# Second layer of a two-layer network: where the softplus pieces, the direct products and TensorE's taps and sums stand among the steps

## The chip, the core and the metric

The kernel runs on one core of one Trainium2 chip. The time is that of one execution on the device, in microseconds (us); of several runs the median is taken. The engines are named as in the profile: PE is TensorE's matmul, PEld its weight load, DVE is VectorE, ACT is ScalarE, POOL is GpSimd, SP is SyncE, which issues the transfers here. Each engine works through its own instructions strictly in the order of the program; engines wait for each other by semaphores.

## What is computed

The input is 16 images of 128 channels with 56 x 56 pixels, all in 32-bit floats. The first layer is a block of window attention and an MLP; the change leaves it alone. The second layer, cut to what matters:

```python
y = conv3x3(x) + conv_b                       # 128 -> 128 channels
seq = y.reshape(B*H*W, 8, 16)                 # 8 tokens of 16 numbers
xi, z = split(seq @ in_proj.T)                # 32 and 32
xc = silu(causal_conv4(xi) + conv1d_b)
dt, Bm, Cm = split(xc @ x_proj.T)             # 1, 16, 16
dt = softplus(dt * dt_proj + dt_proj_b)       # 32
# over the 8 tokens, for 32 channels x 16 states:
h = exp(dt * A) * h + dt * Bm * xc
ys = sum over the states of h * Cm
ym = (ys + D * xc) * silu(z)
out = ym @ out_proj.T
return x + silu(group_norm(out))
```

## The kernel before

**Blocks.** `layer1` cuts each image into 7 blocks of 448 columns, 112 blocks in all, and works on them one after another. A block has 8 tokens and two halves `jp` of its channels, so token 1 to 7 times two halves gives 14 *steps*; the outer loop runs over blocks `i`, the inner over steps `k` from 0 to 13. No scheduler sets the order: the loop at the end of `layer1` issues the instructions, and `_chain` ties every instruction to the one before it on its engine. So the order of the source is the order on every engine.

**The recurrence in each step.** In this order of issue:
- `advance` (DVE): L946 multiplies the decay `a` by the state before, L947 adds the input. For the last token there is one instruction (L944) in place of the two.
- `inject` (DVE, L936): the input of a step 4 ahead, from `x` in PSUM and the gate `bb` in SBUF, into a tile `h`. `h` has four buffers, which are handed out in turn.
- `decay` (PE, L918): the exponent of a step 2 ahead, into one of two PSUM tiles `a`.
- `spread` (PE, L929): the input of a step 5 ahead, into the only PSUM tile `x`.
- `decay_exp` (ACT, L921): the exponential of `a` in place. `advance` two steps later reads it.
- `weigh` (POOL, L951), in odd steps: a token's `h` times the gate `cb`, into one of four tiles `cst`.

**The rest of the work** is dealt out by `work(i, k)`, which returns a list for PE (with the ACT instructions that belong to it), one for DVE and one for POOL; a step issues them after the recurrence, DVE's first, then PE's, then POOL's. `p` is the block at hand, `nxt` the next, `far` the one after that, `prev` the one before, `two` and `three` those two and three blocks back. Two PSUM banks, `pq[0]` and `pq[1]`, serve all of it:
- for `far`: `sequences` (L829, step 11) and `inner` for `xc` (L836, then a table load, two SiLU, and a load back to the table of Exp and Ln, step 12);
- for `nxt`: the rate's softplus in two halves. `rate` (PE L850, ACT L851 and L852), `rate_exp` (ACT L856, L857), `rate_log` (ACT L861, L862) and `rate_sum` (POOL L867 to L870, steps 6 and 8). Then `gate` (PE L876, ACT copies L880, two transfers to memory, step 3), `inner` for `zs` (step 4), `product` (POOL L896, step 10) and `direct` (PE L900), whose result `direct_mul` (DVE, two L905) uses for the first and last token;
- for `p`: `skip` (L966), which opens a sum in `pq[1]`, `gather` (L960, four matmuls for each token), which adds to it, `collect` (DVE L973), `gated` (POOL L976);
- for `prev`: the last gathers, `project_out` (PE L994, ACT copies L1002 and L1005, steps 5 and 6) and `statistics` (DVE L1021; a block with an odd number issues two, one in step 9 and one in step 10 of the block after it);
- for the next image: `convolve`, the 9 *taps* of the 3x3 convolution (L787, accumulated in `pq[0]`, steps 5 to 10), after the last one the copies L796 on ACT;
- once in each image: the group norm. Its variance (PE L1038, ACT L1039 and L1040) comes in step 5 of block 1 of the next image, `normalise` (a load, two long SiLU at L1061, a load) in step 12 of the same block, and the `store` steps on POOL (L1068) with the output transfers after it.

**Transfers.** SP issues them in the order of the program: `bring` reads the gates back, spread over the partitions, as `bb` and `cb`.

Before the change the list for a block reads, in step order: rates in 1 and 2, `rate_exp` in 2 and 3, `rate_log` in 3 and 4, taps 1, 1, 2, 2, 2, 1 in steps 5 to 10, gathers of tokens 1, 2, 3 in steps 8, 9, 10, and in step 13 `skip`, `gather` of token 4 and then `direct`, with `direct_mul` in step 1 of the block after it.

## Time and profile before

| what | value |
|---|---|
| median of 3 runs | 8841.8 us (8837.53 to 8855.01) |
| the profiled execution | 8843.74 us, its span 8841.9 us |
| granted clock of TensorE, mean | 0.966 |
| PE, PEld | 91%, 38% of the span |
| DVE, ACT, POOL | 88%, 63%, 80% of the span |
| second layer, first to last L944/L946 | 3250.8 to 8801.4 us |
| L946 waits for L921 (ACT), in the layer | 357.5 us, 232 times, longest 6.6 |
| L936 waits for L929 (PE) | 141.7 us, 234 times, longest 2.6 |
| L936 waits for the transfer of `bb` | 30.7 us, 12 times, longest 3.1 |

How to read the profile: the span runs from the program's first instruction to its last, on the engines' clocks. A line of a group has the source line, engine and operation, the tiles that it writes and reads, how often it ran, then its busy time and the mean duration of one, and last the idle time of the engine in front of it with what ended that. A line of a timeline has the start and the duration in us, then the same names; "x2" means that two neighbours were merged, and a wait stands in brackets at its end. Neighbours on one engine overlap by up to a tenth of a microsecond. A line of a table of windows has the stretch, its length, the busy time of each engine with its number of instructions, the granted clock, the busy share of the DMA engines and GB/s. A matmul in 32-bit floats shows as two instructions.

### The profile page before, as it was taken

The page shows a single profiled execution, that of the slowest core. Times are in us where ns is not written, and L with a number is a line of the kernel's source. Part 1 is how long each engine was busy: PE and PEld are TensorE (multiplying, and loading weights), DVE is VectorE, ACT ScalarE, POOL GpSimd, SP SyncE. Part 2 cuts the span into 40 slices and gives each one's busy share as a digit, 9 for nine tenths or more (in the row PEclk, how much of TensorE's full clock was granted, in tenths as well). Part 3 has the DMA queues.
Part 4 walks back from the last instruction along what each step waited for, and adds up shares of the span by engine and source line. Part 5 has one row for each costly group of instructions (what it writes and reads, how often), then busy time and mean ns, then how long its engine had stood idle before and what let it go on. Part 6 is the DMA issues. An engine that isn't in the chain of part 4 may idle for free.

```text
span 8841.9 us, 151450 instructions
## 1 busy us (share of the span) xinstructions
PE 8013.1 (91%) x52860; PEld 3322.9 (38%) x52860; DVE 7764.8 (88%) x10358; ACT 5603.8 (63%) x10516; POOL 7035.4 (80%) x5664
## 2 busy tenths in 40 slices
PE   6999999999999879999999999999999999999987
PEld 3444444444444433333333333333333333333332
DVE  7999999999999839898898988988988989889887
ACT  4776777777777636666655665665656665666654
POOL 5878888878888328888888888888888888888887
PEclk8999999999999989999999999999999999999997
DMA  2333333333333222333333333333333333333332
GB/s 62 85 85 89 87 87 87 86 87 89 87 86 88 76 61 80 93 90 83 90 90 83 91 83 99 84 88 93 87 85 86 88 92 91 82 98 85 87 89 69
DMA packets 764424, 757.86 MB, mean 86 GB/s; under 512 B 188688, under 2 KB 663952, under 8 KB 761616
## 3 DMA queue, kind: packets, MB, share of 16 engines
q1 hardware_dynamic: 763664, 748.18, 32.8%
q8 instruction: 422, 6.91, 0.3%
q14 instruction: 338, 2.77, 0.1%
HBM read 439.61 MB, written 102.76 MB: 61 GB/s over the span
## 4 chain that ended last, share of the span: by engine, by line
PE 31%; ACT 24%; DVE 21%; POOL 11%; issue 10%; DMA 1%; SPq 0%; ACTq 0%; POOLq 0%; DVEq 0%
PE pq L787 8%; PE a L918 8%; ACT a L921 5%; DVE a L946 5%; DVE lepe L460 4%; DVE h L947 4%; POOL xh L263 4%; PE pq L960 4%; POOL e L379 4%; PE x L929 3%; ACT L837 3%; DVE h L936 3%; POOL tap L261 2%; ACT L145 2%; DVE sst L363 2%
## 5 line engine op out<-in xcount | busy, mean ns | idle before, releaser
L951 POOL TENSOR_TENSOR cst<-h,cb 128x1792 f32<-128x1792 f32 x784 | 3129.4, 3996 | 855.1 <-DVE h L947 580.4
L921 ACT ACTIVATE a<-a 128x896 f32<-128x896 f32 x1568 | 1404.3, 900 | 1772.7 <-PE x L929 1174.8
L936 DVE TENSOR_TENSOR h<-x,bb 128x896 f32<-128x896 f32 x1568 | 1697.6, 1083 | 276.9 <-PE x L929 145.6
L918 PE MATMUL a<-dt,adec 32*128 32x448 f32 x6272 | 1659.7, 606 | 214.4 <-DVE h L947 213.5
L946 DVE TENSOR_TENSOR a<-a,h 128x896 f32<-128x896 f32 x1344 | 1466.3, 1091 | 358.1 <-ACT a L921 357.5
L460 DVE SCALAR_TENSOR_TENSOR lepe<-vpad,lep,lepe 128x448 f32<-128x448 f32 x2688 | 1718.4, 678 | 0.6
L929 PE MATMUL x<-dtx,amask 32*128 32x448 f32 x6272 | 1664.8, 608 | 25.5 <-DVE h L936 24.5
L947 DVE TENSOR_TENSOR h<-a,h 128x896 f32<-128x896 f32 x1344 | 1467.0, 1092 | 45.8
L379 POOL TENSOR_SCALAR e<-e,sst,zero 128x256 f32<-128x256 f32 x1568 | 861.6, 560 | 451.4 <-DVE sst L375 396.6
L369 ACT ACTIVATE e<-ps,sst 128x256 f32<-128x256 f32 x1568 | 728.8, 469 | 544.5 <-DVE sst L363 493.6
L787 PE MATMUL pq<-x1pad,conv 128*128 128x448 f32 x2016 | 942.8, 580 | 59.5 <-ACT gst L1039 32.5
L918 PEld LDWEIGHTS a<-dt,adec 32*128 32x128 f32 x6272 | 484.2, 188 | 1247.4 <-DVE h L947 578.4
L263 POOL TENSOR_TENSOR xh<-xh,tap 128x448 f32<-128x448 f32 x735 | 841.4, 1145 | 42.5
L960 PE MATMUL pq<-cst,sel 128*32 128x448 f32 x6272 | 750.9, 564 | 1.5 <-POOL cst L951 1.5
L401 PE MATMUL ptt<-ident,e 128*128 128x128 f32 x3136 | 546.4, 285 | 92.3 <-POOL e L379 75.2
L363 DVE TENSOR_REDUCE sst<-ps 128x2 f32<-128x512 f32 x784 | 540.4, 689 | 86.3 <-PE ps L357 63.8
L929 PEld LDWEIGHTS x<-dtx,amask 32*128 32x128 f32 x6272 | 485.0, 189 | 339.8 <-DVE h L936 333.7
L357 PE MATMUL ps<-sel,q 32*64 32x256 f32 x6272 | 540.8, 413 | 68.2 <-ACT e L369 61.7
L261 POOL TENSOR_SCALAR tap<-xpad,pos,zero 128x448 f32<-128x448 f32 x735 | 533.6, 726 | 34.4
L787 PEld LDWEIGHTS pq<-x1pad,conv 128*128 128x128 f32 x2016 | 349.2, 194 | 497.4 <-issue 441.9
L401 PEld LDWEIGHTS ptt<-ident,e 128*128 128x128 f32 x3136 | 367.9, 142 | 416.5 <-POOL e L379 238.0
L407 ACT COPY att<-ptt 128x512 f32<-128x512 f32 x784 | 458.6, 585 | 48.0 <-PE ptt L401 40.3
(164 smaller groups left out, 12292.7 us busy)
## 6 DMA issues: line engine op xcount, KB each, us to landing
sel<-kv SPq DMA_DIRECT2D x3136, 64.0 KB
bb<-db SPq DMA_DIRECT2D x336, 448.0 KB
cb<-dc SPq DMA_DIRECT2D x336, 448.0 KB
xpad<-x SPq DMA_DIRECT2D x32, 784.0 KB
x<-r SPq DMA_DIRECT2D x112, 224.0 KB
x1pad<-x SPq DMA_DIRECT2D x16, 1568.0 KB
db<-bs SPq DMA_DIRECT2D x112, 224.0 KB
dc<-cs SPq DMA_DIRECT2D x112, 224.0 KB
```

The lines of the kernel that those rows point to most:

```text
L263: nc.gpsimd.tensor_add(im["xh"][i], im["xh"][i], held["tap"])
L379: nc.gpsimd.tensor_scalar(e, e, im["st", w][:, 2, p : p + 1], zero, ALU.mult, ALU.add)
L460: nc.vector.scalar_tensor_tensor(out, src, lep[:, k : k + 1], acc, ALU.mult, ALU.add)
L787: nc.tensor.matmul(pc, lhsT=conv[:, k, :], rhs=pad[:, 8 * i + dy : 8 * i + dy + 8, dx : dx + W], start=(k == 0), stop=(k == 8),)
L918: nc.tensor.matmul(a[:, k, :], lhsT=adec[rows, l4, :], rhs=p["dt"][rows, h, :], start=True, stop=True)
L921: nc.scalar.activation(p["a", l, jp], p["a", l, jp], AF.Exp)
L929: nc.tensor.matmul(x[:, k, :], lhsT=mask[rows, l4, :], rhs=p["dtx"][rows, h, :], start=True, stop=True)
L936: nc.vector.tensor_mul(p["h", l][:, own(jp), :], px["x"], weight)
L946: nc.vector.tensor_mul(a, a, before)
L947: nc.vector.tensor_add(p["h", l][:, own(jp), :], a, p["h", l][:, own(jp), :])
L951: nc.gpsimd.tensor_mul(c, p["h", l], p["gate", 1, l].unsqueeze(1).to_broadcast([P, 4, BLK]))
L960: nc.tensor.matmul(py[32 * j : 32 * j + 32], lhsT=sel[:, l4, :], rhs=p["c", l][:, j, :], start=False, stop=(l % 4 == 3), skip_group_check= ...
```

## The change

All of it is in `work`; no instruction is added, removed or resized.

```diff
         if p:
-            if k == 1:
+            if k == 0:
                 dve.append(partial(direct_mul, p))
             if k == 7:
                 pe.append(partial(skip, p, 0))
-            if k in (8, 9, 10):
-                pe.append(partial(gather, p, k - 7))
+            if k in (8, 9, 11):
+                pe.append(partial(gather, p, min(k - 7, 3)))
             if k == 12:
                 dve.append(partial(collect, p, 0))
             if k == 13:
+                if nxt:
+                    pe.append(partial(direct, nxt))
                 pe += [partial(skip, p, 1), partial(gather, p, 4)]
                 pool.append(partial(gated, p, 0))
...
             if k in (1, 2):
                 pe.append(partial(rate, nxt, k - 1))
-            if k in (2, 3):
-                pe.append(partial(rate_exp, nxt, k - 2))
-            if k in (3, 4):
-                pe.append(partial(rate_log, nxt, k - 3))
+            if k in (2, 6):
+                pe.append(partial(rate_exp, nxt, k // 4))
+            if k in (5, 7):
+                pe.append(partial(rate_log, nxt, k // 2 - 2))
...
             if k == 10:
                 pool.append(partial(product, nxt))
-            if k == 13:
+            if k == 13 and not p:
                 pe.append(partial(direct, nxt))
 
         if p and k in (5, 6, 7, 8, 9, 10) and p["b"] + 1 < NB:
-            taps = {5: (0,), 6: (1,), 7: (2, 3), 8: (4, 5), 9: (6, 7), 10: (8,)}[k]
+            taps = {5: (0,), 6: (1, 2), 7: (3,), 8: (4,), 9: (5, 6), 10: (7, 8)}[k]
             pe.append(partial(convolve, p["b"] + 1, p["g"], taps))
```

- The pair `direct_mul` goes from step 1 to step 0 of its block, and `direct` in step 13 ahead of `skip` and `gather`.
- Softplus: the first half's `rate_exp` stays in step 2, the second half's goes from step 3 to 6. `rate_log` goes from steps 3 and 4 to steps 5 and 7. The step with the SiLU of `zs` (4) and the one before it hold no softplus piece any more. `rate_sum` on POOL stays in steps 6 and 8.
- Taps become 1, 2, 1, 1, 2, 2 in steps 5 to 10; the gather of token 3 goes from step 10 to step 11, ahead of `sequences`.
- Inside a step the lists are issued as before. SP's transfers keep their steps and their order.

## The prediction

> **What bounds the kernel now.** I read the page's shares first, then its groups with the idle time in front of them, then the timeline of ScalarE (ACT), VectorE (DVE), GpSimd (POOL) and TensorE (PE) over one block, then busy time by window. The change touches the second layer alone, which runs from 3250.8 us (its first L946) to 8801.4 us, 112 blocks of 14 steps; nothing before is altered.

> ```profile
> PE 8013.1 (91%) x52860; PEld 3322.9 (38%) x52860; DVE 7764.8 (88%) x10358; ACT 5603.8 (63%) x10516; POOL 7035.4 (80%) x5664
> L946 DVE TENSOR_TENSOR a<-a,h 128x896 f32<-128x896 f32 x1344 | 1466.3, 1091 | 358.1 <-ACT a L921 357.5
> ```

> No engine is full. DVE carries the recurrence, and the second line says where it stands still: 357.5 us in front of L946, each time for ACT's exponential of the decay (L921). DVE's waits list adds 141.7 us for PE at L936 and 30.7 us for a DMA. So the layer is DVE's chain plus such waits. The waits sit in two places of each block, as one block shows (4938.94 to 4986.56 us, block 6 of image 4; step 5 begins at 4957.16):

> ```profile
> 4942.92 1.10 DVE L946 TENSOR_TENSOR a<-a,h 128x896 f32<-128x896 f32 x1 [0.76 <-ACT a L921]
> ...
> 4965.04 1.10 DVE L946 TENSOR_TENSOR a<-a,h 128x896 f32<-128x896 f32 x1 [1.54 <-ACT a L921]
> ...
> 4983.02 1.09 DVE L936 TENSOR_TENSOR h<-x,bb 128x896 f32<-128x896 f32 x1 [0.20 <-PE x L929]
> ```
> ```profile
> 4956.69 0.65 ACT L861 ACTIVATE u<-u,neg 128x448 f32<-128x448 f32 x1
> 4957.24 0.56 ACT L862 ACTIVATE ln<-e 128x448 f32<-128x448 f32 x1
> 4957.71 0.51 ACT L880 COPY bs<-pq 128x448 f32<-128x448 f32 x1
> 4958.12 0.53 ACT L880 COPY cs<-pq 128x448 f32<-128x448 f32 x1
> 4958.55 0.92 ACT L921 ACTIVATE a<-a 128x896 f32<-128x896 f32 x1
> 4959.48 1.28 ACT L837 ACT_TABLE_LOAD   x1
> 4960.78 0.98 ACT L837 ACTIVATE zs<-pq 128x448 f32<-128x448 f32 x2
> 4961.77 1.28 ACT L145 ACT_TABLE_LOAD   x1
> 4963.07 0.67 ACT L861 ACTIVATE u<-u,neg 128x448 f32<-128x448 f32 x1
> 4963.64 0.56 ACT L862 ACTIVATE ln<-e 128x448 f32<-128x448 f32 x1
> 4964.11 1.70 ACT L921 ACTIVATE a<-a 128x896 f32<-128x896 f32 x2
> ```

> In step 1 DVE waits 0.76 us behind the SiLU of `xc` (load, two SiLU, load, then the exponential); in step 7 it waits 1.54 us behind the SiLU of `zs`, and there a softplus piece (L861, L862) stands between the second load and the exponential that DVE wants. ACT has no gap from 4956.69 to 4966.

> POOL in the same block:

> ```profile
> 4959.61 3.99 POOL L951 TENSOR_TENSOR cst<-h,cb 128x1792 f32<-128x1792 f32 x1 [1.75 <-DVE h L947]
> 4963.56 1.13 POOL L867 TENSOR_TENSOR u<-u,e 128x448 f32<-128x448 f32 x1
> ...
> 4976.98 4.00 POOL L951 TENSOR_TENSOR cst<-h,cb 128x1792 f32<-128x1792 f32 x1
> ```

> From 4959.61 POOL runs without a gap until past the block's end. L951 of step 9 ends at 4980.98. That matters because `h` has four buffers: the tile that L936 fills in step 12 is the one that this L951 reads. Today L936 starts at 4983.02, 2.0 us later.

> **Part A: direct_mul in step 0, `direct` ahead of skip and gather.** In before, DVE finishes L936 of step 0 at 4942.16, waits 0.76, and does the pair L905 in step 1, where it moves the next L946 by 1.18 us (4946.06 to 4947.24). After, the pair fills the wait: step 1 begins at 4942.08+1.18, about 4943.25, 0.33 later than now, and step 2 at 4943.25+3.13 = 4946.4 against 4947.24. Gain 0.8. It needs `direct` on PE by 4942.1: its bank is free when the first SiLU is read (about 4940.1), PE is done with a and x at 4940.2, L900 takes 0.95 (4942.56 to 4943.51), so it ends near 4941.2. It adds a wait on POOL's product L896, done at 4980.94+1.13, 4 us ahead. L966, now after L900, loses its 0.48 wait for the second SiLU. Rate (L850) no longer waits for L905. After a normalise (block 2 of an image) the wait is 6.65 us, and the whole pair goes under it: gain 1.18.

> **Part B: softplus pieces.** L856/857 of half 1 go from step 3 to 6, L861/862 of half 0 from 3 to 5, of half 1 from 4 to 7: same instructions, three pieces of 1.0 to 1.2 us. The copies L880 come some 1.7 us sooner, but the first load waits for PE's `zs` product, which PE starts at 4958.27 behind its own a and x, so the load moves by 0.1 only. Then 1.30 + 0.99 + 1.30 bring the exponential to 4962.97 in place of 4964.11, and L946 of step 7 to 4963.9: 1.13 of the 1.54 go. [...] **What is late next** is POOL. L867 needs L861, which now ends behind the exponential, near 4964.5 against L867's start at 4963.56: POOL's gapless run starts 0.96 later. 4964.52 + 17.42 (4963.56 to 4980.98) = 4981.94, so L936 of step 12 can't start before about 4982.0; DVE alone would be there at 4981.6 here and 1.05 sooner in blocks without the two L1021. Gain from step 5 to L936 of step 12: 4983.02-4982.0 = 1.0; I take 0.9 over these blocks. The cost of this new wait lies between 0 (DVE not there earlier) and 1.5. Half 1's pieces delay no exponential: a's slack at steps 8 and 9 is over 1 us. SP issues its transfers at the same steps.

> **Part C: taps and gather.** PE's extras by step (tap 0.87, gather 0.89, projection 0.93, skip 0.9, L829 0.6): step 6 1.8 to 2.7, step 7 2.65 to 1.8, step 8 2.6 to 1.8, step 10 1.8 to 1.75, step 11 0.6 to 1.5; the sum is the same. With 0.97 for a and x when they overlap, a step of DVE (3.13) holds 2.16. So only steps 6 and 9 overrun, by half a microsecond each, where three in a row (7, 8, 9) did. This should remove the 0.3 to 0.8 that L936 of step 12 waits for PE, already inside the 0.9 since POOL ends there. The gather in step 11 fills PE's wait for `y` (0.31 at L829); beyond that its 0.89 delays L829, covered by the tap that ends sooner. Bounds: 0 to 0.9 lost.

> **Sum.** Blocks 3 to 6 of an image (64): 0.8+0.9 = 1.7 each, 109. Block 0 (16): its L936 waits more for PE (0.4), 2.1 each, 34. Block 1 (16): there PE stands 2.32 us for L1039, which comes at 5060.51 behind the same softplus piece, and DVE then 2.0 for ACT and 1.3 for PE; 3.5 each, 56.

> ```profile
> 4938.95:4986.40 47.45, 44.93 (x233) 16.06 (x232) 44.55 (x47) 29.46 (x43) 40.13 (x19) 1.00 0.35 93
> ...
> 5034.00:5084.30 50.30, 44.41 (x237) 16.14 (x236) 44.11 (x46) 30.09 (x45) 41.50 (x25) 0.97 0.28 74
> 5084.30:5140.00 55.70, 46.02 (x230) 15.94 (x229) 43.52 (x46) 34.15 (x45) 46.65 (x22) 0.94 0.43 110
> ```

> The columns after the counts are granted clock, DMA share, GB/s: 1.00 in a plain block, 0.97 and 0.94 in blocks 1 and 2, where PE stood idle. [...] Block 2 (15): 1.2 from A; B's gain is mostly eaten by step 8, where L936 waits for the `bb` that queues behind the output transfers (12 waits, 30.7 us); those start when POOL's store ends, which moves with step 3, so 1.7 each, 26. Together 225. The profiled execution took 8843.7 (span 8841.9 and 1.8 around it), 2 above the median of the runs; 8843.7-225 = 8619. I say **8620**.

> **Rivals.** (1) POOL's run does not hold DVE in step 12 (its L861 comes sooner, or DVE is never early): DVE's own chain decides, 1.0 more in some 80 blocks: 8540. For: POOL has 7 us of idle in a block of 47.5. Against: none of it lies between steps 5 and 13. (2) PE stays late at steps 9 to 12 (two doubled steps, then the gather ahead of L829), B's gain is lost there and only A is left: 96 x 0.8 + 16 x 1.2 = 96, 8748. For: PE waits are already there (141.7). Against: steps 7 and 8 get lighter. (3) Slower: POOL's run starts later than I put it, since L867 now hangs on ACT's whole SiLU chain. If L861 comes d after L867's present start, L936 of step 12 comes at 4981.04 + d; A gives 0.8, so above d = 4983.0-4981.0+0.8 = 2.8 (against my 0.96) a block is longer. At d = 3.5, as when each of the two loads cost its 1.28 twice, 0.7 x 80 blocks = 56: 8900. [...] Against: nothing between those instructions shows a gap today.

> **Chances.** Forecast 0.62, (1) 0.10, (2) 0.12, (3) 0.11, and 0.05 for d near its break-even, no change within 0.2% (17 us, about what a measurement of this kernel tells apart). Faster 0.84, same 0.05, slower 0.11. The range goes from 8525, below (1), to 8765, above (2); it leaves out (3), the case of no change and a little below.

> **What would show it.** Right: in front of L946 the wait for ACT falls from 357.5 to about 100 (the normalises stay, some 5 us each); L905 stands in step 0 with no wait; L850's weight load no longer waits for L905; POOL L867 waits about 1 us for ACT L861 in each block; DVE L936 gains a wait for POOL L951 of 0.4 to 1.5 us, and its wait for PE shrinks; plain blocks last 45.8. Wrong: plain blocks of 44.8 without that POOL wait (1), L936 waiting for PE for 100 us or more (2), or L867 waiting over 2.8 us (3).

## The result, and the profile after

The changed kernel takes **8626.7 us** (median of 4 runs, 8623.0 to 8633.6) beside 8841.6 for the kernel before (4 runs, 8837.5 to 8855.0): a ratio of 0.9755, 95% interval 0.9738 to 0.9772. The forecast was 8620. The profiled execution took 8623.8 (span 8621.0), 219.9 less than that of before; the sum of the prediction was 225. In a later set of runs, on another chip, the changed kernel took 8621.2 (the median of five; a sixth run, of 16809 us, is not counted).

The page of the changed kernel, the shares of the span and two of the groups:

```profile
PE 7967.5 (92%) x52860; PEld 3364.3 (39%) x52860; DVE 7747.2 (90%) x10358; ACT 5633.7 (65%) x10516; POOL 7025.6 (81%) x5664
...
L936 DVE TENSOR_TENSOR h<-x,bb 128x896 f32<-128x896 f32 x1568 | 1694.9, 1081 | 298.3 <-PE x L929 172.1
...
L946 DVE TENSOR_TENSOR a<-a,h 128x896 f32<-128x896 f32 x1344 | 1464.1, 1089 | 129.0 <-ACT a L921 127.0
```

The instructions and their durations are those of before (L946 lasts 1089 ns against 1091); only idle time went. In front of L946 it fell from 358.1 to 129.0 us. The 298.3 us in front of L936 hold one wait of 93.6 us at 3241 us, before the layer's first L946, so the waits of VectorE (DVE) within the second layer tell more. Columns: total us, times, longest.

```profile
DVE a L946 <- ACT a L921: 127.0, 128, 6.0
DVE h L936 <- PE x L929: 74.6, 79, 3.3
DVE h L936 <- POOL cst L951: 67.7, 83, 2.4
DVE h L936 <- DMA bb<-db: 48.5, 15, 4.1
DVE h L936 <- POOL gst L1046: 9.8, 3, 3.3
```

Before it was 357.5 for ScalarE (ACT), 141.7 for TensorE (PE), 30.7 for the transfer and nothing to speak of for GpSimd (POOL). So 298 us of waits went, and 95 came back: 67.7 of these are a wait for POOL that was not there.

Block 6 of image 4 again (now 4854.10 to 4899.76; step 5 begins at 4871.45), first VectorE:

```profile
4857.22 1.26 DVE L905 SCALAR_TENSOR_TENSOR ud<-pq,vec,dtx 128x448 f32<-128x448 f32 x2
4858.40 1.08 DVE L946 TENSOR_TENSOR a<-a,h 128x896 f32<-128x896 f32 x1
...
4878.16 1.10 DVE L946 TENSOR_TENSOR a<-a,h 128x896 f32<-128x896 f32 x1 [0.37 <-ACT a L921]
...
4896.23 1.09 DVE L936 TENSOR_TENSOR h<-x,bb 128x896 f32<-128x896 f32 x1 [0.28 <-POOL cst L951]
```

The pair L905 stands in step 0 with no wait in front, and step 1 follows it with none either. In step 7 0.37 us of the wait of 1.54 are left. In step 12 the wait is now for POOL's L951 of step 9. ScalarE and GpSimd in the same block show why:

```profile
4873.63 1.28 ACT L837 ACT_TABLE_LOAD   x1 [1.08 <-PE pq L836]
4874.93 0.98 ACT L837 ACTIVATE zs<-pq 128x448 f32<-128x448 f32 x2
4875.93 1.28 ACT L145 ACT_TABLE_LOAD   x1
4877.22 0.90 ACT L921 ACTIVATE a<-a 128x896 f32<-128x896 f32 x1
4878.03 0.66 ACT L861 ACTIVATE u<-u,neg 128x448 f32<-128x448 f32 x1
```
```profile
4878.77 1.14 POOL L867 TENSOR_TENSOR u<-u,e 128x448 f32<-128x448 f32 x1 [0.90 <-ACT u L861]
...
4892.20 3.99 POOL L951 TENSOR_TENSOR cst<-h,cb 128x1792 f32<-128x1792 f32 x1
```

ScalarE's table load now stands 1.08 us until the product of `zs` (L836) is there; the exponential follows the second load at once, and the softplus piece L861 comes behind it. POOL's L867 waits for that piece. From 4878.77 POOL runs 17.42 us without a gap to 4896.19, and 0.04 us later L936 of step 12 starts.

Busy time by window, a plain block, block 1 and block 2 of image 5, the same blocks as in the prediction:

```profile
4854.10:4899.76 45.66, 45.16 (x233) 16.45 (x232) 44.59 (x47) 28.85 (x42) 40.12 (x19) 1.00 0.39 101
4945.49:4995.22 49.73, 46.83 (x237) 17.73 (x236) 43.74 (x46) 30.04 (x45) 42.75 (x26) 0.90 0.28 75
4995.22:5051.29 56.07, 46.47 (x234) 16.34 (x232) 44.88 (x48) 35.35 (x46) 48.09 (x23) 0.91 0.44 110
```

The plain block went from 47.45 to 45.66. Block 1 gained only 0.6 here, at a granted clock of 0.90 (0.97 before). The mean lengths over all images, from the start of one block's first L946 to the next's, in us:

| kernel | blocks 3-6 | block 0 | block 1 | block 2 | block 1s with a half-clock stretch |
|---|---|---|---|---|---|
| before | 47.46 | 48.19 | 51.02 | 57.93 | 15 of 16 |
| after | 45.84 | 45.87 | 48.45 | 55.35 | 12 of 16 |
| A alone | 46.77 | 47.62 | 49.81 | 58.06 | 15 of 16 |
| B alone | 46.34 | 46.66 | 48.92 | 56.63 | 8 of 16 |
| C alone | 47.71 | 48.21 | 51.15 | 58.66 | 15 of 16 |
| A and B | 45.71 | 45.67 | 47.43 | 55.68 | 4 of 16 |

From before to after that is 1.62 x 64 = 104, 2.32 x 16 = 37, 2.57 x 16 = 41 and 2.58 x 15 = 39, 221 together. The last column counts blocks with at least 1 us of granted clock at one half; more on it below. The first image's block 1 has no group norm before it, and no such stretch in any kernel.

### The profile page after: what moved, and what is told of

Same layout as the page of the kernel before. It is cut to its first block, busy times and chain, and to the rows that moved or that the text cites. A ratio compares the mean times of both kernels' runs of the same rounds, so it can differ in the third digit from the quotient of the medians.

```text
span 8621.0 us, 151466 instructions
## 1 busy us (share of the span) xinstructions
PE 7967.5 (92%) x52860; PEld 3364.3 (39%) x52860; DVE 7747.2 (90%) x10358; ACT 5633.7 (65%) x10516; POOL 7025.6 (81%) x5664
## 5 line engine op out<-in xcount | busy, mean ns | idle before, releaser
L951 POOL TENSOR_TENSOR cst<-h,cb 128x1792 f32<-128x1792 f32 x784 | 3126.5, 3994 | 523.3 <-DVE h L947 409.6
L921 ACT ACTIVATE a<-a 128x896 f32<-128x896 f32 x1568 | 1416.6, 904 | 1360.2 <-PE x L929 692.6
L936 DVE TENSOR_TENSOR h<-x,bb 128x896 f32<-128x896 f32 x1568 | 1694.9, 1081 | 298.3 <-PE x L929 172.1
L929 PE MATMUL x<-dtx,amask 32*128 32x448 f32 x6272 | 1652.5, 603 | 51.5 <-DVE h L936 43.8
L946 DVE TENSOR_TENSOR a<-a,h 128x896 f32<-128x896 f32 x1344 | 1464.1, 1089 | 129.0 <-ACT a L921 127.0
L947 DVE TENSOR_TENSOR h<-a,h 128x896 f32<-128x896 f32 x1344 | 1467.2, 1092 | 46.1
L787 PE MATMUL pq<-x1pad,conv 128*128 128x448 f32 x2016 | 949.0, 583 | 45.0 <-DMA x1pad<-x 18.7
L929 PEld LDWEIGHTS x<-dtx,amask 32*128 32x128 f32 x6272 | 486.1, 188 | 358.1 <-DVE h L936 327.7
L787 PEld LDWEIGHTS pq<-x1pad,conv 128*128 128x128 f32 x2016 | 349.0, 194 | 471.3 <-issue 430.7
```

Of the source, the lines that this page charges most:

```text
L787: nc.tensor.matmul(pc, lhsT=conv[:, k, :], rhs=pad[:, 8 * i + dy : 8 * i + dy + 8, dx : dx + W], start=(k == 0), stop=(k == 8),)
L921: nc.scalar.activation(p["a", l, jp], p["a", l, jp], AF.Exp)
L929: nc.tensor.matmul(x[:, k, :], lhsT=mask[rows, l4, :], rhs=p["dtx"][rows, h, :], start=True, stop=True)
L936: nc.vector.tensor_mul(p["h", l][:, own(jp), :], px["x"], weight)
L946: nc.vector.tensor_mul(a, a, before)
L947: nc.vector.tensor_add(p["h", l][:, own(jp), :], a, p["h", l][:, own(jp), :])
```

## The experiments

The theory is that of the prediction: A fills VectorE's wait in step 1, B takes the softplus piece out from between the second table load and the exponential for step 7, and then POOL's run from L867 sets step 12; C is worth about nothing. The runs were made in three sets, each on one chip (an expectation below says "call" for a set); the kernel before took 8854.1 us in the first set (13 runs), 8852.4 in the second (7) and 8851.5 in the third (11).

### First set: each part alone, and A with B

**A alone.** `direct_mul` in step 0, `direct` ahead of `skip` and `gather` in step 13:

```diff
-            if k == 1:
+            if k == 0:
                 dve.append(partial(direct_mul, p))
...
             if k == 13:
+                if nxt:
+                    pe.append(partial(direct, nxt))
                 pe += [partial(skip, p, 1), partial(gather, p, 4)]
...
-            if k == 13:
+            if k == 13 and not p:
                 pe.append(partial(direct, nxt))
```

> The kernel before with part A alone (direct_mul in step 0, direct ahead of skip and gather in step 13); softplus, taps and gathers as before. My theory, each part takes out its own wait and the gains add up: 0.8 us in 96 blocks and 1.2 in 16, 96 us, 8746 us; step 2 begins 7.5 us after step 0, and the 1.5 us wait for ACT in step 7 stays as it is. Rival, the two waits are one lateness that travels on: what is won in step 1 is waited for again in step 7 or 12, and the time is over 8810.

Measured: 8785.0 us (8772.6 to 8790.4), ratio 0.9939 [0.9917, 0.9960]; 69 less than before, between the two expectations: neither the 96 of the theory nor the rival's loss of most of it. VectorE's waits over the second layer:

```profile
DVE a L946 <- ACT a L921: 278.5, 141, 5.5
DVE h L936 <- PE x L929: 150.4, 243, 2.1
```

From step 0 to step 2 a plain block takes 7.44 us in place of 8.24: the 0.8 is there. But step 7 waits 1.62 for ScalarE in place of 1.51, so that 0.69 is left at the block's end: a part of the lateness did travel on, as the rival has it, but a small one. In block 2 step 2 comes 1.17 sooner as well (12.62 against 13.79 us after the start), but steps 2 to 5 then take 11.46 in place of 10.44, with 1.46 us of waiting for TensorE in front of L936 in step 3: the gain is given back there.

**B alone.** The pieces of the softplus in other steps:

```diff
-            if k in (2, 3):
-                pe.append(partial(rate_exp, nxt, k - 2))
-            if k in (3, 4):
-                pe.append(partial(rate_log, nxt, k - 3))
+            if k in (2, 6):
+                pe.append(partial(rate_exp, nxt, k // 4))
+            if k in (5, 7):
+                pe.append(partial(rate_log, nxt, k // 2 - 2))
```

> The kernel before with part B alone (softplus pieces in steps 2, 6 and 5, 7). My theory: L946 of step 7 comes 1.13 us sooner, L936 of step 12 then waits for POOL and comes 0.9 to 1.0 sooner; 80 blocks at 0.9, block 1 of an image 1.7 and block 2 about 1.4 each: about 8842 - 122 = 8720, with a wait of L936 for POOL L951. Rival, B needs C: with the old taps PE is late in steps 9 to 12, L936 waits for PE there as before, B gives under 0.4 a block and the time is over 8790.

Measured: 8690.8 us (8688.7 to 8698.8), ratio 0.9829 [0.9808, 0.9850]: 163 less than before, more than the theory gave.

```profile
DVE a L946 <- ACT a L921: 196.0, 221, 6.6
DVE h L936 <- PE x L929: 88.2, 132, 2.5
DVE h L936 <- POOL cst L951: 66.8, 88, 4.0
```

The new wait for POOL comes with B alone, without A or C. In plain blocks (3 to 6 of an image) step 7's wait is down to 0.37 us, step 12 waits 0.67 for POOL where TensorE held it 0.47 in A alone, and the block is 1.12 shorter. So B does not need C. Blocks 0, 1 and 2 gain more: 1.5, 2.1 and 1.3.

**C alone.** The order of taps and the gather of token 3:

```diff
-            if k in (8, 9, 10):
-                pe.append(partial(gather, p, k - 7))
+            if k in (8, 9, 11):
+                pe.append(partial(gather, p, min(k - 7, 3)))
...
-            taps = {5: (0,), 6: (1,), 7: (2, 3), 8: (4, 5), 9: (6, 7), 10: (8,)}[k]
+            taps = {5: (0,), 6: (1, 2), 7: (3,), 8: (4,), 9: (5, 6), 10: (7, 8)}[k]
```

> The kernel before with part C alone (taps 1, 2, 1, 1, 2, 2, the gather of token 3 in step 11). My theory: C is worth nearly nothing by itself. It removes the 0.3 to 0.5 us that L936 of step 12 waits for PE and brings xc's SiLU 0.4 us later, which step 1 pays back: 8842 within 25. Rival, C carries a share of its own: under 8800. Other rival, the later gather costs: over 8870.

Measured: 8866.2 us (8857.4 to 8873.8, 10 runs), ratio 1.0015 [1.0000, 1.0029]: no gain; the 12 us of loss can only just be told apart from none. VectorE's wait for TensorE falls from 141.7 to 105.2 us, its wait for ScalarE rises from 357.5 to 412.4: what C takes off one, the other takes back. Step 2 comes 8.76 us after step 0 in place of 8.24, since the gather in step 11 delays the SiLU of `xc` (from 4.08 to 4.62 us behind L936 of step 12), and with it the exponential for step 1.

**A and B, without C.**

> Parts A and B with the taps and gathers of before. My theory, C is worth nearly nothing here too: 8627 within 20, plain blocks of 45.8 us, set by POOL's run at L936 of step 12. Rival, C is what lets PE keep up once DVE goes faster: L936 waits for PE by 0.5 us or more in most blocks, and the time is over 8665.

Measured: 8605.8 us (8598.2 to 8611.5), ratio 0.9736 [0.9715, 0.9757]. The expected time was about that of the changed kernel, within 20; it is 21 below it, but on another chip. C is certainly not needed: in step 12 of the plain blocks no wait of L936 for TensorE is left. The wait for POOL is 70.2 us here too.

### Second set: the halves of C, and POOL's start

**A, B and the gather in step 11** (first half of C):

> Parts A and B, and of part C only the gather of token 3 in step 11 (taps 1, 1, 2, 2, 2, 1 as before). Parts A and B alone took 8606, all three 8627. My theory: the gather ahead of the transposes makes xc's SiLU come 0.3 to 0.6 us later against L936 of step 12, so that the exponential of step 1 ends level with direct_mul; plain blocks then cost up to 0.15 us more, block 1 of an image costs nothing more: 8606 to 8616. Rival, the later gather is all of C's cost: 8622 or more.

Measured: 8616.9 us (8607.5 to 8632.9), ratio 0.9741 [0.9724, 0.9758]. Plain blocks cost 0.14 us more than with A and B (45.85) and block 1 nothing more (47.20), as the theory has it; the time is 1 us above its range.

**A, B and the new taps** (second half of C):

> Parts A and B, and of part C only the taps (1, 2, 1, 1, 2, 2; the gather of token 3 stays in step 10, which now holds a gather and two taps). My theory: the second tap of step 6 falls into block 1 of an image, where PE is late after the group norm's variance, and costs about 1 us there, 16 in all; the plain blocks wait a little more for PE in step 11 or 12, 0.1 to 0.3 each: 8622 to 8645. Rival, the taps are free: under 8612.

Measured: 8618.6 us (8604.5 to 8631.6), ratio 0.9742 [0.9726, 0.9758]. The time lies between the two expectations, and the theory's reason is not there: block 1 takes 47.09 us, with no extra microsecond. Neither half brings block 1 to the 48.45 us of the changed kernel (47.20 with the gather alone): both together do.

**A and B, with the first L861/862 back in step 3.** If POOL's run in the changed kernel starts late because L867 waits for L861, this piece ahead of the SiLU should set it free:

```diff
-            if k in (5, 7):
-                pe.append(partial(rate_log, nxt, k // 2 - 2))
+            if k in (3, 7):
+                pe.append(partial(rate_log, nxt, k // 4))
```

> Parts A and B, but the first half's rate_log in step 3 as before (the second half's pieces stay in steps 6 and 7). ACT has some 2 us free between the exponential of step 3 and the first load, so the load should not move. My theory, POOL's run decides: L867 starts 0.95 us sooner, L951 of step 9 ends 23.8 us after step 5 begins and not 24.8, the wait of L936 for POOL (70 us now) falls under 20; then PE or DVE itself decides, 0.35 to 0.5 us a block sooner: 8575, 8565 to 8590. Rival, POOL's wait is only where a lateness shows that PE has too: 8600 or more. Other rival, the load comes later again: over 8620.

Measured: 8628.7 us (8623.4 to 8650.7), ratio 0.9757 [0.9738, 0.9776]. A miss: 54 us above the expected time. VectorE's waits for POOL's L951 are gone, 70.2 us to 1.3, since L867 starts 6.40 us after step 5 begins in place of 7.33. But right behind that wait stood another, as the first rival had it (the second is out, as the load comes 2.19 us after step 5 begins in both):

```profile
DVE h L936 <- PE x L929: 146.3, 227, 2.2
```

In step 12 of a plain block L936 now waits 0.46 us for TensorE where it waited 0.68 for POOL: the block is 45.53, 0.18 shorter, and not the 0.35 to 0.5 that I had expected. And blocks 1 and 2 are longer, 48.26 and 57.45 us.

**The changed kernel with the same piece in step 3:**

> All three parts (the changed kernel), but the first half's rate_log in step 3. My theory: the wait of L936 for POOL goes here too, but with the gather in step 11 xc's SiLU is bound to PE and does not move with it, so step 1 waits for ACT by what step 12 gained: 8615, 8595 to 8627, with a wait of 0.3 to 0.9 us for ACT in step 1. Rival, the gain is the same as without C: under 8595.

Measured: 8616.0 us (8602.8 to 8620.0), ratio 0.9729 [0.9713, 0.9746]. Plain blocks 45.35 us, the shortest of all kernels, the wait for POOL 13.6 us; but block 1 49.21 and block 2 56.56. The time is the theory's, but not for its reason: the 0.3 to 0.9 us of waiting for ScalarE in step 1 is 0.04. In plain blocks C's new order of TensorE's work has a use after all once POOL no longer binds, and blocks 1 and 2 take it back.

### Third set: C side by side, the buffer, and `direct`

> The change without Part C a second time, beside the changed kernel on the same chip, since their times so far come from different chips. Theory (the gather of token 3 in step 11 and the new taps cost something, mostly in block 1 of an image, where the mean block is 48.45 us with them and 47.43 without): 15 to 30 us below the changed kernel of this call. Rival (Part C costs nothing, as predicted, and the difference was the chips'): within 8 us of it.

> The changed kernel a second time, as the other side of that comparison: 8610 to 8640 by both theories.

Measured: A and B 8599.4 us (8597.6 to 8611.5, 5 runs), ratio 0.9721 [0.9700, 0.9742]; the changed kernel 8621.2 (8618.2 to 8630.8, 5 runs), ratio 0.9742 [0.9721, 0.9763]. On one chip the runs of the two do not overlap: **C costs 22 us**, as the theory of this pair had it. By the table, of earlier executions: 0.13 x 64 = 8 in plain blocks, 0.2 x 16 = 3 in block 0, 1.02 x 16 = 16 in block 1, less 0.33 x 15 = 5 in block 2.

Where block 1 loses it, one image shows. TensorE in steps 5 to 8 of block 1 of image 5, with A and B, and then in the changed kernel:

```profile
4968.74 1.02 PE L787 MATMUL pq<-x1pad,conv 128*128 128x448 f32 x2 [1.28 <-ACT gst L1039]
...
4970.65 1.03 PE L994 MATMUL pq<-wo,ym 128*128 128x64 f32 x8
```
```profile
4969.74 1.86 PE L787 MATMUL pq<-x1pad,conv 128*128 128x448 f32 x2 [1.28 <-ACT gst L1039]
...
4973.34 1.74 PE L994 MATMUL pq<-wo,ym 128*128 128x64 f32 x8
```

The same wait of 1.28 us for L1039, then the same instructions, 1.82 times (L787) and 1.69 times (L994) as long in the changed kernel: after this wait the granted clock is one half there, 1.00 in the other. Windows of block 1 with A and B:

```profile
4944.49:4991.25 46.76, 43.67 (x237) 16.22 (x236) 43.87 (x45) 30.67 (x46) 41.23 (x25) 1.00 0.29 79
```

Counted over all images, block 1 with A and B runs into such a stretch in 4 of 16 images, in both executions; in the changed kernel in 12 of 16, in both. Without it block 1 takes 46.66 us with A and B and 46.48 in the changed kernel, with it 49.75 and 49.10. So C's own work costs nothing in block 1; the halved clock does.

The length of the wait does not tell these images apart. In the eleven traces of kernels with Part B, whole or in part, it is 1.27 or 1.28 us in all 154 places. Its place does: in these traces half clock begins and ends on a grid of boundaries 3.413 us apart (last section). In 85 places the wait began 0.97 to 2.97 us after such a boundary, and half clock followed each time from the next boundary on; in the other 69 it began 0.00 to 0.82 or 2.99 to 3.41 us after one, and half clock followed in none; of the 14 places of the changed kernel's first trace the 11 with half clock lie at 2.12 to 2.97 us, the 3 without at 0.21, 0.25 and 3.04. In the image shown it began 3.30 us after a boundary with A and B and 2.90 in the changed kernel. From one image's wait to the next it is 331.0 us with A and B where no stretch came between (the median), 97.0 times 3.413, so that a good place is kept for several images; 331.2 and 331.4 with either half of C. In the changed kernel it is 330.2 us (330.6 in its second trace), which brings the next wait 0.5 to 0.9 us earlier against the boundaries, out of a good place, and with a stretch 334.4, 98.0 times 3.413, which keeps a bad one. By these figures, what C costs in block 1 comes from the length that it gives an image. This is read from the traces; no run moved the wait alone.

The miss of the second set has the same in it: with the piece in step 3 block 1 is 45.99 without such a stretch, 0.67 shorter, but 11 of 16 have one; block 2 holds 12.8 us of half clock, against 10.9 and 12.1 in the two executions of A and B.

**Five buffers for `h`, three for `cst`** (A and B):

```diff
+    w5 = ctx.enter_context(tc.tile_pool(name="l1w5", bufs=5))
...
-            p["h", l] = w4.tile([P, 4, BLK], F32, tag="h", name=f"h_{p['n']}_{l}")
+            p["h", l] = w5.tile([P, 4, BLK], F32, tag="h", name=f"h_{p['n']}_{l}")
...
-        c = p["c", l] = w4.tile([P, 4, BLK], F32, tag="cst", name=f"cst_{p['n']}_{l}")
+        c = p["c", l] = w3.tile([P, 4, BLK], F32, tag="cst", name=f"cst_{p['n']}_{l}")
```

> The change without Part C, with five buffers for h in place of four and three for cst in place of four. Theory (L936 of step 12 waits for GpSimd's L951 of step 9 because both go by the same one of the four buffers of h): VectorE's wait for POOL in step 12, 0.68 us a plain block, falls below 0.1, and the wait for TensorE that stands right behind it, 0.46 us in the run with the exponential's pieces apart, takes part of its place: plain blocks 45.3 to 45.6 us, time 8580 to 8606. Rival (the wait is for something else that GpSimd has to do first, or three buffers of cst hold GpSimd up as long): plain blocks stay at 45.7 or above, 8606 or more.

Measured: 8663.0 us (8655.9 to 8681.0), ratio 0.9795 [0.9769, 0.9821]. The lines stand one further down in this kernel, so that L937 is L936:

```profile
DVE h L937 <- PE x L930: 153.3, 239, 2.1
...
DVE h L937 <- DMA bb<-db: 76.0, 24, 5.7
DVE h L937 <- POOL cst L952: 8.0, 5, 1.9
```

The wait for POOL in step 12 is gone although L951 of step 9 ends 3.4 us later than with A and B (28.11 us after step 5 begins, against 24.76): **it was the buffer**. Plain blocks are 45.58 us, as expected. The time is not: block 1 is 1.4 and block 2 2.6 us longer than with A and B (11 of 16 half-clock stretches, 13.7 us of half clock in block 2, waits for `bb` 76.0 us against 45.8). So the theory was right on the wait and wrong on the time, which falls to the rival's side without the rival's reason in the plain blocks. How much of that is POOL's later end by the three buffers of `cst` and how much the clock, this run does not separate.

**`direct` left last in step 13** (A and B otherwise):

> The change without Part C, and with the product of L900 left at the end of TensorE's step 13, behind skip and gather; only its multiplication (L905) is in step 0. Theory (L905 needs that product, which would end 4.2 to 4.6 us after step 0 starts, while VectorE reaches L905 about 3.1 us after it): L905 waits 1.1 to 1.5 us in 96 blocks, 105 to 145 us in all: 8710 to 8750. Rival (TensorE reaches the product early enough, so that it need not go ahead): L905 waits under 0.4 us, 8606 to 8645.

Measured: 8777.5 us (8774.7 to 8785.0), ratio 0.9922 [0.9897, 0.9948].

```profile
DVE ud L905 <- PE pq L900: 146.7, 111, 3.7
```

The wait is what the theory says, 1.31 us in a plain block; 1.3 x 112 blocks is 147. The time is above the theory's 8710 to 8750: it is 178 above A and B, 30 more than the wait. Block 1 is 2.35 longer, with 14 of 16 half-clock stretches, and blocks 4 and 5 now have such a stretch in 9 and 13 images (in one each with A and B). With a ratio of 0.9922 this kernel is even slower than B alone (0.9829): `direct_mul` one step sooner is a loss unless its product goes ahead too.

## Why the prediction was right

**What is late next.** This step carried the forecast, and it held to a tenth of a microsecond. Taken from the start of step 5 in a plain block: L867 at 7.33 us (put at 6.40 + 0.96), POOL's run 17.42 (17.42), L936 of step 12 at 24.80 (put at 24.85; before 25.75). L867 waits 119.9 us in 120 places for L861, about 1 a block as forecast, and L936 67.7 us in 83 places for L951, 0.8 each. That this is the buffer of `h`, the run with five buffers shows; that it comes from L861's place, the run with the piece in step 3 and B alone. What the prediction did not see: TensorE stands about 0.2 us behind POOL. Rival (1) priced POOL's release at 1.0 a block; released, a plain block gains 0.13 to 0.18 with A and B, 0.49 with C as well.

**Part A** was put at 0.8 a plain block. From step 0 to step 2 it is 0.80 (A alone, and A with B), 0.72 in the changed kernel, where C delays the exponential; at the end of the block 0.63 (on top of B) to 0.69 (alone). With A alone the wait in step 7 grows by 0.11 and takes the rest. In block 2 the 1.18 of A alone is lost by step 5.

**Part B** was put at 0.9 and is 1.06 to 1.12. In step 7 0.37 us of wait are left (forecast 0.41), and the table load moved by 0.13 (forecast 0.1), because L836 holds it. In the changed kernel's second layer each table load took its 1.28 us once; the next instruction follows 472 of the 475 loads within 0.02 us and the other three within 0.08, and the second load follows the SiLU within 0.02 us. So the two loads add nothing beyond the 1.28 us each, and L867 waits 1.5 us for L861 at the longest, where rival (3) needed 2.8.

**Part C** was put at 0, with a bound of 0.9 lost a block. It costs 22 us, 0.2 a block in the mean, three quarters of it by the clock in block 1, which the step-by-step count of Part C could not show. The cover named for the gather in step 11, TensorE's wait for `y`, does not cover it wholly either: the SiLU of `xc` comes later.

**Blocks 1 and 2** are the terms that were mis-sized. Block 1 was to save 3.5 and saved 2.57; block 2 was to save 1.7 and saved 2.58, since B alone already gives 1.3 there. The two errors cancel by luck: 56 + 26 forecast, 41 + 39 measured. It is luck of the same kind that the whole comes so near: by the table A and B without C save about 243, more than the 225, and C takes 22 of it. In block 1 the shorter idle did come, TensorE's wait for L1039 fell from 2.32 to 1.28 us in each of the 14 images that have it, but the half clock went in 3 of 15 images only. Before the change half clock followed the wait of 2.32 us in all 14; after it, half clock followed the wait of 1.28 us in 11 of the 14. With A and B the stretch went in 11 of 15 images, in the changed kernel not.

**The rivals.** (2), TensorE late in steps 9 to 12, would have shown 100 us or more of L936 waiting for TensorE; it is 74.6, and plain blocks have 0.02 of it in step 12. (1) and (3) are answered above. Plain blocks at 45.84 are the 45.8 forecast.

**What stays open.** Why half clock followed the wait of 1.28 us at some places between two boundaries and not at others; and no run shows that a kernel with C would be rid of the stretches if its images were a little longer. TensorE's idle time in block 1 is the same with C (2.85 us) as without (2.98). A version clearly better than A and B was not found: the changed kernel with the piece in step 3 has a ratio of 0.9729 [0.9713, 0.9746], A and B 0.9736 and 0.9721, in different sets.

## What to carry to other kernels

Before you price the removal of a wait, look up who is second at the same instruction, and third: here POOL stood 1.0 us behind ScalarE's wait and TensorE 0.2 behind POOL, and the second place was worth almost nothing once free. An instruction moved forward needs its producer moved too; the multiplication without its product took 178 us more than with it. And where half clock follows an idle time of 1.28 us in some images and not in others, as here, small moves elsewhere can weigh more than the work they shift: with C that idle time came 0.5 to 0.9 us earlier against the boundaries from image to image, and 12 block 1s in place of 4 had a half-clock stretch. So read the granted clock block by block before you put a difference down to the instructions.

## What the runs showed of the hardware

In the changed kernel a table load carries the wait of the activation behind it: in the block shown L837's load starts only after 1.08 us of waiting for L836's product, which the SiLU reads (the load's line names no tile), so the load was not hidden under that wait. In the layer ScalarE waits so in 110 places, 105.7 us in all.
